# Four graph-attention layers on one core: a bias that rides in with the features, and masks and maxima made for all heads at once

## The chip, the cores and the metric

The kernel runs on one core of a Trainium2 chip. The metric is device time in microseconds of one execution; three timed runs of the kernel before gave 3248.8, 3250.99 and 3244.18 us, median 3248.8. A profile of one execution of the same program shows when each engine was at work: PE (matrix products, with its weight loads PEld), DVE (the vector engine), ACT (pointwise functions), POOL, and SP, whose queue issues nearly all DMAs.

## The reference

128 graphs of 128 nodes with 512 features, and an adjacency matrix for each, pass four graph-attention layers. Each layer normalises and clips its input, and adds its output to it:

```python
h = jnp.maximum(_layernorm(x, axis=-1), 0.0)
x = x + layer(h, adj)
```

All layers score a pair of nodes by a leaky ReLU of the sum of two per-node numbers, mask by the adjacency, take a softmax and sum the nodes' features with it. Layer 1 is two such attentions in a row: the first has 4 heads of 256 features, then a bias and an elu, and the second has one head of 512:

```python
h = jax.nn.elu(gat_layer(x, mask, W1, att_src1, att_dst1, b1, concat=True))
h = gat_layer(h, mask, W2, att_src2, att_dst2, b2, concat=False)
```

Here `gat_layer` returns the attention-weighted sum of `xl = x @ W` plus the bias, and the attention weights of a node sum to 1. Layer 3 has 8 heads of 64 features and a ReLU at the end. All numbers are fp32.

## The kernel before

The 128 graphs are independent, and each is a stream of steps (`graph(b)`, line 1033): layer 0, 1, 2 and 3, then the store. Up to 13 streams are in flight. The program's order is made before the run by the kernel's own planner (`Scheduler`, lines 154 to 312): it holds an estimate of each step's time (`Step.estimate`, line 66), looks for the engine that could start something first, and issues on it the ready step of lowest rank; a rank is the graph's number times the pace plus the step's due time (line 242). A step waits in the planner where its stream needs a buffer that no other has given back (`Take`), where a fork is not over (`Join`), or where a name has not been reached (`Until`). On the chip, each engine then runs its own instructions strictly in that order. A `Group` is a set of instructions of one engine that are issued together.

`setup()` (line 428) loads the weights. Small vectors come by ACT's queue (`few`, line 424), all else by SP's. `fold_w1` (line 516) works out columns of `w1x` that give the scores of layer 1 along with its features; `fold_w2` (line 522) does the same for `w2x` by 16 dot products on DVE, and `fold_w3` for layer 3. `b2` holds layer 1's second bias, spread over all partitions, and is added when the second projection is taken out of PSUM.

Layer 1 (`layer1`, line 797): the clipped input is transposed on PE and copied out by ACT (`ht`). `projected` (line 741) multiplies it by `w1x` in three parts of 344 columns, each of four 128-row chunks; ACT copies each part out of its PSUM bank into `fx` (tile tag `xl`), whose first 8 columns are the scores. When `plus` is given, `projected` has DVE add a row to the part on the way out; before, only the second projection does that, with `b2`. After the softmax, each group of four 128-row pieces of the output (`po`, a PSUM bank) has four matmuls. Then `y` is made from it (lines 852 to 866) in four steps: DVE adds the bias `b1` (one number a partition and piece), which frees the bank; DVE takes the minimum with 0 into a tile `t`; ACT takes the exponential; and DVE takes the maximum of that less 1 and the sum. There are two such groups a graph. `y` is then the left operand of the second projection by `w2x`, in two parts of 257 columns with eight chunks each.

Layer 3 (`layer3`, line 891): a tile `e` of 128 x 1024 holds the scores of 8 heads. For each head one DVE instruction adds the mask and takes the row's maximum into `mx` (lines 928 to 942, two groups of four). POOL and ACT make the softmax's offset from `mx`, and ACT then runs two functions over each head. In the last 5 graphs (`late`) the rows come from PE transposes in PSUM, four heads at a time; in the others by DMA. At the end `t` collects the normalised output.

A matmul of fp32 is two PE instructions with a weight load each. PSUM is 8 banks (`bank`); tile tag `t` has five buffers and is used by layer 0 from its dots to its end, by layer 1 for each group of `y`, by layer 3 at its end, and by `fold_w3`.

Of the kernel before, what the change touches and what calls it, by code (L numbers as in the profile page):

```python
# [9 lines left out]
F32 = mybir.dt.float32  # L10
# [143 lines left out]
class Scheduler:  # L154
# [14 lines left out]
    def give_back(self, *aps):  # L169
        for ap in aps:  # L170
            name = ap.tensor.name
            tag = self.tag_of.pop(name)
            heapq.heappush(self.returned[tag], self.last_use.get(name, 0.0))
# [153 lines left out]
def kernel(  # L327
# [23 lines left out]
    nc = tc.nc  # L351
# [60 lines left out]
    w_src = const.tile([P, D], F32, name="w_src")  # L412
    w_dst = const.tile([P, D], F32, name="w_dst")
    b_l2 = const.tile([P, 1], F32, name="b_l2")
    b1 = const.tile([P, FC], F32, name="b1")
    u1 = const.tile([P, D], F32, name="u1")
    u2 = const.tile([P, D], F32, name="u2")

# [5 lines left out]
    def few(to, values):  # L424
        with nc.allow_non_contiguous_dma(reason="at most 1024 values, once"):
            nc.scalar.dma_start(out=to, in_=values)

    def setup():
        for i, a in enumerate((l0_a1, l0_a2)):
            few(a0[:, :, i], a.rearrange("(c p) o -> p (c o)", p=P))  # L430
        for i, a in enumerate((l1_src1, l1_dst1)):
            few(a1[:, :, i], a.rearrange("h (c p) -> p (h c)", p=P))
        few(b1, l1_b1.rearrange("(c p) -> p c", p=P))

        w0 = []
        for c in range(KC):
            if c % 2 == 0:
                pair = yield tile_of("e3", 3, H3 * P)
                pair = pair.rearrange("p (c f) -> p c f", c=2)
            w0.append(pair[:, c % 2])  # L440
            yield S.dma_start(out=w0[c], in_=l0_w[c * P : (c + 1) * P])
        yield Fork(fold_u(w0))
        yield from load(0)
        for c in range(KC):
            yield S.dma_start(out=w1x[c][:, E1:], in_=l1_w1[c * P : (c + 1) * P])
        yield Fork(fold_w1())
        yield Fork(load_turned(0))
        yield from load(1)
        yield from load(2)
        vecs = []  # L450
        for row in (l1_src2, l1_dst2):
            vecs.append((yield tile_of("x2", 2, E2 + D))[:, :D])
            yield S.dma_start(out=vecs[-1], in_=row[0].partition_broadcast(P))
        for c in range(FC):
            yield S.dma_start(out=w2x[c][:, E2:], in_=l1_w2[c * P : (c + 1) * P])
        yield Fork(fold_w2(vecs), 3)
        yield S.dma_start(out=b2[:, E2:], in_=l1_b2.partition_broadcast(P))
        yield from load(3)
        yield from load(4)
        for t, row in (w_src, l2_src), (w_dst, l2_dst), (b_l2, l2_b), (b_l3[:, 0], l3_batt):  # L460
            yield S.dma_start(out=t, in_=row.partition_broadcast(P))
        yield from load(5)
        for c in range(KC):
            yield S.dma_start(
                out=wpx[c][:, :, E3:],
                in_=l3_wp[c * P : (c + 1) * P].rearrange("p (h k) -> p h k", h=H3),
            )
        wa = yield tile_of("e3", 3, H3 * P)
        wa = wa[:, : H3 * 2 * K3]
        yield S.dma_start(out=wa, in_=l3_watt.rearrange("h k -> (h k)").partition_broadcast(P))  # L470
        yield Fork(fold_w3(wa), 6)
        for b in range(6, min(FLYING + AHEAD, B)):
            yield from load(b)
# [42 lines left out]
    def fold_w1():  # L516
        for w in w1x:
            to = w[:, :E1].rearrange("p (s h) -> p h s", h=H1)
            yield from fold(blocks_of(w[:, E1:]), a1, F1 // P, to)
        sched.reached.add("w1")  # L520

    def fold_w2(vecs):
        for w in w2x:
            for s, vec in enumerate(vecs):
                yield from dot(w[:, E2:], vec, w[:, s : s + 1])
        give_back(*vecs)
        sched.reached.add("w2")

    def fold_w3(wa):
        pairs = wa.rearrange("p (h k) -> p h k", h=H3)  # L530
        for w in wpx:
            for s in range(2):
                prod = yield tile_of("t", 5, D)
                p3 = prod.rearrange("p (h k) -> p h k", h=H3)
                yield V.tensor_tensor(
                    p3, w[:, :, E3:], pairs[:, :, s * K3 : (s + 1) * K3], ALU.mult
                )

                yield V.tensor_reduce(w[:, :, 1 - s], p3, AX.X, ALU.add)
                give_back(prod)  # L540
        give_back(wa)
        sched.reached.add("wp")
# [31 lines left out]
    def blocks_of(t):  # L574

        return [t[:, i : i + P] for i in range(0, t.shape[1], P)]
# [202 lines left out]
    def layer0(xt, mask, late):  # L779
        h = yield from norm_relu(xt)  # L780
        yield Until("u")
        f = yield tile_of("f0", 8, 3)
        yield from dot(h, u1, f[:, 0:1])
        yield from dot(h, u2, f[:, 1:2])
        t = yield tile_of("t", 5, D)
        pa, c, rz = yield from attended(f[:, 0:1], f[:, 1:2], mask, h, late, exact=True)
        give_back(h, f)

        yield A.activation(out=t, in_=pa, func=AF.Exp, scale=rz)
        yield A.activation(out=pa, in_=pa, func=AF.Relu, scale=rz)  # L790
        give_back(c)
        yield V.scalar_tensor_tensor(t, t, 1.0, pa, ALU.min, ALU.add)
        give_back(pa)
        yield V.scalar_tensor_tensor(xt, t, -1.0, xt, ALU.add, ALU.add)
        give_back(t)

    def layer1(xt, mask, late):
# [18 lines left out]
                d = yield from rows_in_dram(fx[:, :Q], H1)  # L816
                yield S.dma_start(out=e.rearrange("p (c f) -> p c f", c=R), in_=d)

        fork = yield from projected(ht, KC, w1x, 3, columns(fx, 3), rows)
        give_back(ht[0])  # L820
        xl = fx[:, E1:]
        yield Join(fork)
# [15 lines left out]
        for g in range(0, FC, 4):  # L838
            po = yield bank()
            yield Group(  # L840
                [
                    T.matmul(
                        po[:, (c - g) * P : (c - g + 1) * P],
                        lhsT=xl[:, c * P : (c + 1) * P],
                        rhs=et[c * P // F1],
                        start=True,
                        stop=True,
                    )
                    for c in range(g, g + 4)
                ]  # L850
            )
            yg = y[:, g : g + 4, :]
            yield V.tensor_tensor(
                yg,
                po.rearrange("p (j q) -> p j q", q=P),
                b1[:, g : g + 4].unsqueeze(2).to_broadcast([P, 4, P]),
                ALU.add,
            )
            give_back(po)

            yg = yg.rearrange("p c q -> p (c q)")
            t = yield tile_of("t", 5, 4 * P)
            yield V.tensor_scalar(t, yg, 0.0, None, ALU.min)
            yield A.activation(out=t, in_=t, func=AF.Exp)
            yield V.scalar_tensor_tensor(yg, t, -1.0, yg, ALU.add, ALU.max)
            give_back(t)
        give_back(fx, et[0])
        yield Until("w2")
        gx = yield tile_of("x2", 2, E2 + D)
# [21 lines left out]
    def layer3(xt, mask, late):  # L891
# [27 lines left out]
            yield S.dma_start(out=e.rearrange("p (c f) -> p c f", c=R), in_=rows)  # L919
        mask3 = mask.rearrange("p (c b) -> p c b", b=Q)  # L920

        for g in range(0, H3, 4):
            part = [heads[:, g + j] for j in range(4)]
            if late:
                pt = yield from spread(f[:, 0, g : g + 4])
                part = pt.rearrange("p (h c b) -> p h c b", h=4, b=Q)
                part = [part[:, j] for j in range(4)]
            yield Group(
                [
                    V.tensor_tensor_reduce(  # L930
                        out=heads[:, g + j],
                        in0=part[j],
                        in1=mask3,
                        scale=1.0,
                        scalar=LOWEST,
                        op0=ALU.add,
                        op1=ALU.max,
                        accum_out=mx[:, g + j : g + j + 1],
                    )
                    for j in range(4)  # L940
                ]
            )
            if late:
                give_back(pt)
        give_back(mask)
        yield G.tensor_tensor(mx, mx, f[:, 1], ALU.add)
        yield A.activation(out=mx, in_=mx, func=AF.Prelu, alpha=SLOPE)
# [10 lines left out]
        else:  # L958
# [5 lines left out]
            )  # L964
            give_back(to)
            et = blocks_of(e)
        t = yield tile_of("t", 5, D)
        for i in range(2):
            pa = yield bank()
            p3 = pa[:, : half * (K3 + 1)].rearrange("p (h k) -> p h k", h=half)  # L970
# [28 lines left out]
    def load(b):  # L999

        xs[b] = xpool.tile([P, D], F32, tag="xt", name="xt")
        yield S.dma_start(out=xs[b], in_=x[b])
        if b % AG == 0:
            adjs[b // AG] = adjp.tile([P, AG, P], I32, tag="at", name="at")
            yield S.dma_start(
                out=adjs[b // AG], in_=adj[b : b + AG].rearrange("g i j -> i g j")
            )
            if b:
                yield Fork(load_turned(b))
        sched.reached.add(("x", b))  # L1010
# [117 lines left out]
```

## Time and profile before

| | |
|---|---|
| timed runs, median (lowest to highest) | 3248.8 us (3244.18 to 3250.99) |
| span of the profiled execution; no other time of it is given | 3245.8 us |
| PE busy | 3191.5 us, 98% |
| DVE busy | 2865.8 us, 88% |
| ACT busy | 2468.6 us, 76% |
| POOL busy | 861.3 us, 27% |
| granted TensorE clock, mean | 0.988 |
| DMA | 462.80 MB, 143 GB/s |

The span runs from the first to the last instruction of the program. Matmuls are pipelined and their ends are modelled, so two that follow each other overlap in the records; the distance of their starts tells what one costs. The same holds for DVE and ACT: an instruction's record overlaps the next one's by some 0.1 us. All the kernel's steps are issued from one line of the planner, 302, so groups of instructions are told apart by the names of the tiles that they write and read, not by the line.

### The profile page before, as it was taken

Reading aid. Unit: us, or ns where it says so; the run is one execution under the profiler, and the core shown is the slowest. Engines: PE = TensorE matmul, PEld = TensorE weight load, DVE = VectorE, ACT = ScalarE, POOL = GpSimd, SP = SyncE. Lnnn points to the kernel's source line nnn. Section 1 sums busy time; section 2 is a strip of 40 time slices with the busy share of each in tenths; the row PEclk is TensorE's granted clock in tenths of the full one; section 3 lists DMA queues with packets and bytes.
Section 4 is the critical chain, followed back from the end, with each engine's and each line's share of the span. In section 5 each row is a group of like instructions: output and inputs, shape, how many; then the busy total and the mean of one; then the engine's idle time right before and its main releaser. Section 6 shows DMA issues by size and latency. Waiting matters only on the chain.

```text
span 3245.8 us, 60294 instructions
## 1 busy us (share of the span) xinstructions
PE 3191.5 (98%) x15362; PEld 2498.0 (77%) x15362; DVE 2865.8 (88%) x11669; ACT 2468.6 (76%) x7221; POOL 861.3 (27%) x2313
## 2 busy tenths in 40 slices
PE   6999999999999999999999999999999999999998
PEld 3777777777777777777777777777777777777786
DVE  5788989999999999989989989989989989989876
ACT  3567777777777777777777778777778777777867
POOL 1122222222222222222222222222222222222222
PEclk6999999999999999999999999999999999999999
DMA  6235565555555555555656555556565555565432
GB/s 172 65 87 141 145 156 146 153 150 149 146 153 151 154 151 147 147 154 151 152 147 153 145 156 152 150 148 154 143 158 152 145 149 154 145 156 149 113 98 69
DMA packets 774259, 462.80 MB, mean 143 GB/s; under 512 B 345496, under 2 KB 706200, under 8 KB 773912
## 3 DMA queue, kind: packets, MB, share of 16 engines
q1 hardware_dynamic: 769736, 458.94, 54.3%
q8 instruction: 123, 2.02, 0.3%
q14 instruction: 224, 1.84, 0.2%
q10 hardware_dynamic: 4176, 0.02, 0.1%
HBM read 300.57 MB, written 158.17 MB: 141 GB/s over the span
## 4 chain that ended last, share of the span: by engine, by line
PE 94%; DVE 2%; DMA 2%; ACT 1%; issue 1%; SPq 0%; POOL 0%; ACTq 0%; DVEq 0%; POOLq 0%
PE bank L302 94%; DVE e L302 1%; ACT e L302 0%; DMA e<-d 0%; SPq L302 0%; DVE t L302 0%; DVE products L302 0%; DVE st L302 0%; DMA xt<-in_x_dram 0%; DVE xt L302 0%; DMA w1x<-in_L_gnn_W_dram 0%; POOL st L302 0%; DVE y L302 0%; ACT h L302 0%; DMA at<-in_adj_dram 0%
## 5 line engine op out<-in xcount | busy, mean ns | idle before, releaser
L302 PE MATMUL bank<-w2x,y 128*128 128x257 f32 x4096 | 968.7, 381 | 0.5 <-DVE y L302 0.5
L302 PE MATMUL bank<-w1x,ht 128*128 128x344 f32 x3072 | 953.4, 454 | 2.6 <-ACT ht L302 2.6
L302 PEld LDWEIGHTS bank<-w2x,y 128*128 128x128 f32 x4096 | 763.4, 190 | 152.8 <-issue 30.7
L302 PEld LDWEIGHTS bank<-w1x,ht 128*128 128x128 f32 x3072 | 571.5, 191 | 260.4 <-issue 13.8
L302 ACT ACTIVATE e<-e,f 128x128 f32<-128x128 f32 x2176 | 707.8, 390 | 5.8 <-POOL st L302 3.0
L302 POOL TENSOR_SCALAR st<-st 128x1 f32<-128x1 f32 x1024 | 312.7, 310 | 1196.3 <-DVE st L302 1019.5
L302 ACT ACTIVATE e<-e,c 128x128 f32<-128x128 f32 x1408 | 534.3, 394 | 113.4 <-DVE c L302 57.5
L302 PE MATMUL bank<-wpx,ht 128*128 128x264 f32 x2048 | 497.1, 386 | 0.3 <-ACT ht L302 0.3
L302 ACT ACTIVATE h<-xt,st 128x512 f32<-128x512 f32 x512 | 411.0, 810 | 77.2 <-POOL st L302 70.5
L302 PEld LDWEIGHTS bank<-wpx,ht 128*128 128x128 f32 x2048 | 387.9, 190 | 98.7 <-issue 23.0
L302 DVE CUSTOM_DVE_ANT_0 e<-e,m 128x128 f32<-128x128 f32 x1496 | 340.5, 285 | 18.1 <-DMA e<-d 17.7
L302 DVE BATCH_NORM_STATS2 st<-xt 128x6 f32<-128x512 f32 x512 | 341.0, 679 | 0.0
L302 POOL TENSOR_TENSOR st<-st,minus_half 128x1 f32<-128x1 f32 x512 | 297.3, 599 | 23.6 <-POOL st L302 0.2
L302 PEld LDWEIGHTS bank<-x,e 128*128 128x128 f32 x1968 | 255.2, 191 | 58.1 <-issue 33.3
L302 PEld LDWEIGHTS bank<-et,xl 128*128 128x128 f32 x2048 | 265.1, 192 | 36.0 <-issue 9.6
L302 PE MATMUL bank<-h,et 128*128 128x512 f32 x512 | 266.6, 604 | 4.2 <-ACT et L302 3.0
L302 PE MATMUL bank<-et,xl 128*128 128x128 f32 x2048 | 269.4, 275 | 0.3 <-DMA et<-exchanged 0.3
L302 ACT COPY xl<-bank 128x344 f32<-128x344 f32 x384 | 167.8, 437 | 116.9 <-PE bank L302 113.8
L302 PE MATMUL bank<-x,e 128*128 128x65 f32 x1968 | 246.4, 268 | 4.9 <-issue 4.9
L302 ACT COPY ht<-bank 128x512 f32<-128x512 f32 x274 | 159.8, 583 | 117.3 <-PE bank L302 116.3
L302 ACT ACTIVATE t<-t 128x512 f32<-128x512 f32 x256 | 160.3, 626 | 96.3 <-DVE t L302 95.4
L302 DVE TENSOR_TENSOR y<-bank,b 128x512 f32<-128x512 f32 x256 | 175.3, 685 | 37.7 <-PE bank L302 37.0
(83 smaller groups left out, 4344.6 us busy)
## 6 DMA issues: line engine op xcount, KB each, us to landing
e<-d SPq DMA_DIRECT2D x123, 512.0 KB
exchanged<-e SPq DMA_DIRECT2D x492, 128.0 KB
et<-exchanged SPq DMA_DIRECT2D x123, 512.0 KB
xt<-in_x_dram SPq DMA_DIRECT2D x128, 256.0 KB
e<-d SPq DMA_DIRECT2D x128, 256.0 KB
out_dram<-xt SPq DMA_DIRECT2D x128, 256.0 KB
exchanged<-e SPq DMA_DIRECT2D x492, 64.0 KB
et<-exchanged SPq DMA_DIRECT2D x123, 256.0 KB
```

Source lines behind the costliest of these rows:

```text
L302: method(*args, **kw)
```

## The change

The bias of layer 1 is added to the features while they are taken out of PSUM, as `b2` is in the second projection; since the attention weights of a node sum to 1, it comes through the weighted sum unchanged. `b1` therefore becomes a row over all partitions, with zeros where the score columns lie. To it 1 is added once, so that the weighted sum is one more than the argument of the elu. From the PSUM bank ACT takes the exponential of the sum less 1, and one DVE instruction takes the larger of the sum and of the exponential capped at 1: this is the elu plus 1. The bank is given back after that instruction. What the 1 adds to the second projection, the column sums of `w2x`, is worked out once on PE by a product with a matrix of ones, and subtracted from `b2`; the name `w2` is reached after that.

In layer 3, one DVE instruction adds the mask to all eight heads (four at a time, from PSUM, in the last 5 graphs), and one reduction then takes all maxima. Tile tag `t` has four buffers in place of five.

```diff
-    b1 = const.tile([P, FC], F32, name="b1")
+    b1 = const.tile([P, E1 + HF], F32, name="b1")
+    nc.gpsimd.memset(b1[:, :E1], 0.0)
+    minus_one = const.tile([P, 1], F32, name="minus_one")
+    nc.gpsimd.memset(minus_one, -1.0)
+    ones = const.tile([P, 1], F32, name="ones")
+    nc.gpsimd.memset(ones, 1.0)
...
-        few(b1, l1_b1.rearrange("(c p) -> p c", p=P))
...
             yield S.dma_start(out=w1x[c][:, E1:], in_=l1_w1[c * P : (c + 1) * P])
+        yield S.dma_start(out=b1[:, E1:], in_=l1_b1.partition_broadcast(P))
         yield Fork(fold_w1())
...
         yield S.dma_start(out=b2[:, E2:], in_=l1_b2.partition_broadcast(P))
+        sched.reached.add("b2")
...
             yield from fold(blocks_of(w[:, E1:]), a1, F1 // P, to)
+        yield V.tensor_scalar(b1[:, E1:], b1[:, E1:], 1.0, None, ALU.add)
         sched.reached.add("w1")
...
         give_back(*vecs)
+        yield Until("b2")
+        for to, *parts in zip(columns(b2, 2), *(columns(w, 2) for w in w2x)):
+            total = yield bank()
+            for g in range(0, FC, 4):
+                yield Group(
+                    [
+                        T.matmul(
+                            total[:, : to.shape[1]],
+                            lhsT=ones.to_broadcast([P, P]),
+                            rhs=parts[c],
+                            start=(c == 0),
+                            stop=(c == FC - 1),
+                        )
+                        for c in range(g, g + 4)
+                    ]
+                )
+            yield V.tensor_tensor(to, to, total[:, : to.shape[1]], ALU.subtract)
+            give_back(total)
         sched.reached.add("w2")
...
-        t = yield tile_of("t", 5, D)
+        t = yield tile_of("t", 4, D)
...
-        fork = yield from projected(ht, KC, w1x, 3, columns(fx, 3), rows)
+        fork = yield from projected(ht, KC, w1x, 3, columns(fx, 3), rows, plus=columns(b1, 3))
...
-            yg = y[:, g : g + 4, :]
-            yield V.tensor_tensor(
-                yg,
-                po.rearrange("p (j q) -> p j q", q=P),
-                b1[:, g : g + 4].unsqueeze(2).to_broadcast([P, 4, P]),
-                ALU.add,
-            )
-            give_back(po)
-
-            yg = yg.rearrange("p c q -> p (c q)")
-            t = yield tile_of("t", 5, 4 * P)
-            yield V.tensor_scalar(t, yg, 0.0, None, ALU.min)
-            yield A.activation(out=t, in_=t, func=AF.Exp)
-            yield V.scalar_tensor_tensor(yg, t, -1.0, yg, ALU.add, ALU.max)
-            give_back(t)
+            t = yield tile_of("t", 4, 4 * P)
+            yield A.activation(out=t, in_=po, func=AF.Exp, bias=minus_one)
+            yg = y[:, g : g + 4, :].rearrange("p c q -> p (c q)")
+            yield V.scalar_tensor_tensor(yg, t, 1.0, po, ALU.min, ALU.max)
+            give_back(po, t)
...
-        for g in range(0, H3, 4):
-            part = [heads[:, g + j] for j in range(4)]
+        for g in range(0, H3, 4 if late else H3):
+            n = 4 if late else H3
+            own = part = heads[:, g : g + n].rearrange("p h c b -> p c h b")
             if late:
                 pt = yield from spread(f[:, 0, g : g + 4])
-                part = pt.rearrange("p (h c b) -> p h c b", h=4, b=Q)
-                part = [part[:, j] for j in range(4)]
-            yield Group(
-                [
-                    V.tensor_tensor_reduce(
-                        out=heads[:, g + j],
-                        in0=part[j],
-                        in1=mask3,
-                        scale=1.0,
-                        scalar=LOWEST,
-                        op0=ALU.add,
-                        op1=ALU.max,
-                        accum_out=mx[:, g + j : g + j + 1],
-                    )
-                    for j in range(4)
-                ]
-            )
+                part = pt.rearrange("p (h c b) -> p c h b", h=4, b=Q)
+            wide = mask3.unsqueeze(2).to_broadcast([P, R, n, Q])
+            yield V.tensor_tensor(own, part, wide, ALU.add)
             if late:
                 give_back(pt)
+        yield V.tensor_reduce(mx, heads, AX.XY, ALU.max)
         give_back(mask)
```

More of the change, by code (lines that the diff above doesn't have):

```diff
@@ L532, in fold_w3 @@
             for s in range(2):
-                prod = yield tile_of("t", 5, D)
+                prod = yield tile_of("t", 4, D)
                 p3 = prod.rearrange("p (h k) -> p h k", h=H3)
@@ L966, in layer3 @@
             et = blocks_of(e)
-        t = yield tile_of("t", 5, D)
+        t = yield tile_of("t", 4, D)
         for i in range(2):
```

## The prediction

> **What bounds the kernel now.** I read the page's busy table and slices first, to see whether one engine is full all the way, then busy time by stretch, then who PE waits for, then the costliest groups, and last the timeline where PE is not full.
>
> ```profile
> span 3245.8 us, 60294 instructions
> PE 3191.5 (98%) x15362; PEld 2498.0 (77%) x15362; DVE 2865.8 (88%) x11669; ACT 2468.6 (76%) x7221; POOL 861.3 (27%) x2313
> PE   6999999999999999999999999999999999999998
> PEclk6999999999999999999999999999999999999999
> PE 94%; DVE 2%; DMA 2%; ACT 1%; issue 1%; SPq 0%; POOL 0%; ACTq 0%; DVEq 0%; POOLq 0%
> ```
>
> PE is at nine tenths or more in every slice but the first and the last, and the chain that ended last is 94% PE. Busy PE alone proves little, so the starts have to be looked at: between 310 and 3180 us matmuls of one kind start at a fixed distance (217 ns for 257 columns, 289 ns for 344), and the sum of such distances over all matmuls is 3177 us. The other 69 us of the span are at its two ends. The stretches show it (columns: length, then busy time and instructions of each engine, clock, DMA share, GB/s):
>
> ```profile
> 0.00:43.00 43.00, 34.76 (x121) 24.65 (x121) 16.53 (x58) 13.41 (x27) 4.01 (x18) 0.70 1.02 304
> 43.00:76.00 33.00, 10.84 (x22) 4.47 (x22) 28.25 (x86) 10.40 (x22) 7.51 (x20) 0.50 0.17 27
> 76.00:106.00 30.00, 26.68 (x90) 16.98 (x90) 18.38 (x59) 18.00 (x54) 4.53 (x13) 0.90 0.20 50
> 106.00:310.00 204.00, 199.83 (x934) 154.60 (x932) 168.90 (x665) 137.10 (x404) 49.73 (x120) 1.00 0.38 99
> 310.00:3180.00 2870.00, 2867.78 (x13903) 2255.55 (x13904) 2596.19 (x10633) 2242.30 (x6569) 782.46 (x2102) 1.00 0.57 148
> 3180.00:3246.00 66.00, 51.57 (x298) 41.70 (x297) 37.55 (x172) 47.36 (x147) 13.02 (x40) 0.92 0.16 57
> ```
>
> In 2870 us PE is idle 2.2 us; DVE, third column of the five, is idle 274 us and ACT 628 us. Only the first 106 us and the last 66 us leave PE anything to wait for. From 43 to 76 us PE has 10.8 us of work, at half clock, and DVE 28.3 of 33. So the question of this change is whether PE gets more work, whether the start or the end grows, and whether DVE still feeds PE in the middle.
>
> **The change part by part.** Its own units are these rows of the groups:
>
> ```profile
> L302 PE MATMUL bank<-w2x,y 128*128 128x257 f32 x4096 | 968.7, 381 | 0.5 <-DVE y L302 0.5
> L302 DVE SCALAR_TENSOR_TENSOR y<-t,y 128x512 f32<-128x512 f32 x256 | 176.0, 688 | 9.8 <-ACT t L302 6.0
> L302 DVE TENSOR_TENSOR y<-bank,b 128x512 f32<-128x512 f32 x256 | 175.3, 685 | 37.7 <-PE bank L302 37.0
> L302 ACT COPY xl<-bank 128x344 f32<-128x344 f32 x384 | 167.8, 437 | 116.9 <-PE bank L302 113.8
> L302 DVE TENSOR_SCALAR t<-y 128x512 f32<-128x512 f32 x256 | 107.8, 421 | 3.9
> L302 DVE TENSOR_TENSOR x<-bank,b 128x257 f32<-128x257 f32 x256 | 105.0, 410 | 19.6 <-PE bank L302 16.4
> ```
>
> Records of one engine overlap, so I price by the median distance of starts where instructions follow without a gap: bias add on y 0.603 us, minimum 0.338, closing instruction 0.602 (0.658 for the same kind with a PSUM operand, row xt<-bank,c,xt), 257-wide add from PSUM 0.323, ACT copy of 344 0.342, Exp of 512 0.536 from SBUF and 0.586 from PSUM with a column operand. The masks of layer 3 are told by the timeline:
>
> ```profile
> 3229.75 0.29 DVE L302 CUSTOM_DVE_ANT_0 e<-bank,m 128x128 f32<-128x128 f32 x1 [1.89 <-PE bank L302]
> 3229.97 0.08 DVE L302 DVE_READ_ACCUMULATOR2_ANT f<- 128x1 f32 x1
> 3229.97 0.28 DVE L302 CUSTOM_DVE_ANT_0 e<-bank,m 128x128 f32<-128x128 f32 x1
> ```
>
> One starts 0.21 us after the other, accumulator read included.
>
> *Layer 1, per graph.* Removed from DVE: 2 x (0.603 + 0.338 + 0.602) = 3.09 us. Added: 2 x 0.658 = 1.32, and three 344-wide adds from PSUM, between 0.323 at 257 and 0.603 at 512, on the line 0.42 each, 1.26. ACT loses 3 x 0.342 and gains 2 x 0.05: 0.93 less.
>
> *Layer 3, per graph.* Removed: 8 x 0.212 = 1.70 us. Added: one add over 1024 and one reduction over 1024. At 512 both kinds take 0.60 (t<-wpx,e and its reduction wpx<-t); the 1024-wide transpose takes 1.16. Two of these are 2.33 us, so layer 3 gets 0.63 us dearer: eight instructions that added and took the maximum in one pass become two passes.
>
> The Trainium skill, "VectorE: DVE Perf Modes", under "Rules for kernel authors", says to cut the number of DVE instructions, which would make eight into two a gain; the same table says to expect a reduction at its slowest rate and to restructure. The rows decide for the second: by the first rule alone this part would save something of the 1.70 us, by the rows it costs 0.63.
>
> *DVE together:* 3.09 + 1.70 out, 1.32 + 1.26 + 2.33 in: +0.12 us per graph, 15 us over 128. It is spread over 2870 us in which DVE idles 274. I cost it at zero in the middle; the cover is PE's queue of other graphs' work, and without it 15 us would show. The new adds wait for PE at the head of DVE's queue, as x<-bank,b does now (16.4 us for 256); behind them are other graphs' masks and norms. In exchange the wait on y (37.0) moves to ACT, and the wait of r on ACT's xl (46.6) becomes DVE's own order.
>
> *Buffers.* A bank of the 8 is held from its first matmul to its last reader; for the y groups that is 2.8 us on average, and becomes about 4.5 (matmuls 1.0, wait 1.05, Exp 0.68, wait 1.03, closing 0.73). All groups together hold about two banks at a time now; this adds 0.13. Tile t goes from five buffers to four: counted along the timeline never more than four are in use, and four for 3.6% of the time. Both zero.
>
> *Two sums of w2x's rows on PE, once.* 2 halves x 8 chunks x 2 passes = 32 matmuls of 257 columns. At full clock 16 take 3.47 us (118.96 to 122.43 in the timeline), so 6.9 us; at half clock, which 43 to 76 us has, 13.8. They can start when the last dot of w2x is done at 51.7 us, and their result is wanted by the first w2x matmul at 112.3. PE idles 22 us between 43 and 76, so I take zero, and keep 0 and 13.8 as ends.
>
> The Trainium skill, "TensorE: Matmul & The Clock Gate", Part 1, puts the return to full clock at about 3.4 us of sustained work; the trace has 2.9 us from 75.8 and 3.8 us from 95.3. By the page's figure the sums would take about 8.6 us, an estimate.
>
> *Start, DMAs and DVE.* b1 becomes a 512 KB broadcast on SP's queue behind w1x, ahead of at_t, x(1), x(2) and w2x; the small transfer on ACT's queue goes (1.85 us of issue, nobody waits). Up to 43 us the DMA engines are full at 304 GB/s: 1.7 us for everything behind, and the chain runs through DMAs until 46 us, so I take 1.7 (ends 0 and 1.7). DVE gets one pass over b1's 1024 (0.338 at 512, so about 0.7) and two subtractions (0.323 each) in or ahead of a stretch where it is 86% busy: 1.35 (ends 0 and 1.35). Each subtraction waits for its sum at the head of DVE's queue, with layer 0 and at_t's transposes behind it. Between 0 and twice 3.5 us (the half clock's surplus on 16 matmuls) I take 1.0, near the low end, since DVE has 5 us idle there anyway; this wait is the same cost as the 13.8 seen from DVE, not a further end.
>
> *End.* In the last graph the masks of layer 3 run 3229.75 to 3231.5, 1.75 us; two adds of 0.6 and the reduction of 1.15 make 2.35: +0.6 (ends 0 and 1.5, were two graphs' delays to add up). Layer 1 is over by 3176 us, so its shorter chain is worth nothing here.
>
> *Sum:* 1.7 + 1.35 + 1.0 + 0.6 = 4.65 us on a span of 3245.8, 3250.5. The page gives no other time of that execution; the three timed runs have median 3248.8, 3.0 above the span. On that footing I predict 3253.5, 0.14% more. About 0.2%, 6.5 us, is what can be told from no change.
>
> **The rivals.**
> *The sums are not hidden* (slower). The groups of eight matmuls stand in front of the short transposes and products of layer 0 in PE's in-order queue, and DVE stalls behind its subtractions, so that layer 1 starts later than 75.8 us. For it: PE's queue is fixed before the run, and the clock is at half there. Against: 22 us idle. Price 6.9 to 13.8 in place of my 1.0: 3259.4 to 3266.3. It decides as soon as 2.9 us of them show.
> *DVE no longer feeds PE* (slower). 90.5% busy between 310 and 3180 becomes 91%, with 384 evacuations from PSUM more. If a tenth of ACT's 113.8 us of waits for them came through to PE, 11.4 us: 3264.9. Against: PE's waits there are 3.1 us in all with 274 us of DVE idle.
> *The start gets shorter* (faster). at_t's transposes come at 69.2 us though its transfers were issued by 50; another order of DVE's queue could have layer 1 begin up to some 10 us earlier, and the shorter chain of y could take the 4.2 us that PE idles from 106 to 310. All of it would give 3239.3, half 3246.4. Against: nothing in the change touches those steps' own needs.
>
> **How the numbers follow.** Forecast 0.48, sums shown 0.34, DVE 0.06, shorter start 0.12. Slower by over 0.2%: most of the second, the third, a little of the first, 0.38; faster: most of the last, 0.10; within: 0.52. The low end is the 4.2 us gained and nothing lost, 3244.6; the high end all upper bounds, 1.7 + 1.35 + 13.8 + 1.5 = 18.35, 3267. The forecast's own range is 3249 to 3257.
>
> **What the changed profile would show.** Right: 32 more matmuls with w2x as the moving operand, between 52 and 76 us; PE in the middle stretch as full as now; DVE busy 2880 us, ACT 2350; the first stretch of full PE beginning some 4 us later; the reduction at about 1.2 us. Wrong: PE idle in slices 4 to 39, by DVE xl or ACT t; the w1x matmuls starting later than 82 us; an order that brings layer 1 before 70 us; 1024-wide instructions at more than 1.3 us.

## The result, and the profile after

The changed kernel takes 3333.3 us (median of 4 runs, 3324.8 to 3335.9) where the kernel before takes 3248.0 (4 runs, 3244.2 to 3251.0): 1.0256 times as long, 95% interval 1.0239 to 1.0272. The prediction was 3253.5 with a range to 3267.0. It was wrong by about 80 us, and outside its range.

The page of the changed kernel answers the first fence of the prediction:

```profile
span 3333.4 us, 58253 instructions
PE 3231.8 (97%) x15394; PEld 2506.3 (75%) x15394; DVE 2866.1 (86%) x9757; ACT 2304.5 (69%) x6837; POOL 832.5 (25%) x2316
PE   7999999999999999999999999999999999999998
PEclk7999999999999999999999999999999999999999
PE 29%; DVE 29%; DMA 29%; SPq 5%; ACT 3%; issue 3%; POOL 2%; DVEq 0%; ACTq 0%; POOLq 0%
```

Two lines look nearly unchanged, and one has turned over. PE is still at "nine tenths or more" in the same slices, and DVE's busy time is 2866.1 us where it was 2865.8. But the chain that ended last was 94% PE and is now 29% PE, 29% DVE and 29% DMA. A slice of 83 us prints a 9 when PE loses 2 us of it; losses of that size, in most slices, are the result. Busy time by stretch shows where (columns: length, then busy time and instructions of PE, PEld, DVE, ACT and POOL, clock, DMA share, GB/s):

```profile
0.00:43.00 43.00, 32.85 (x121) 22.84 (x122) 15.69 (x56) 12.48 (x28) 4.10 (x21) 0.74 1.01 305
43.00:76.00 33.00, 18.34 (x50) 9.52 (x49) 29.03 (x89) 10.67 (x21) 6.81 (x19) 0.71 0.26 41
106.00:310.00 204.00, 200.33 (x920) 155.20 (x919) 159.56 (x565) 126.08 (x372) 48.50 (x118) 0.98 0.40 96
310.00:3180.00 2870.00, 2813.87 (x13468) 2186.70 (x13467) 2531.64 (x8678) 2036.17 (x6057) 733.54 (x2048) 1.00 0.56 145
3180.00:3333.00 153.00, 139.09 (x735) 113.58 (x734) 103.83 (x289) 101.48 (x311) 33.64 (x96) 0.93 0.24 76
```

From 310 to 3180 us PE did 13468 matmuls where it did 13903, and was idle 56 us where it was idle 2. To see the loss without the overlap of records I took the distance from each matmul's start to the next, less the median distance of its kind in the whole kernel. Summed by stretch, this excess went from 44.5 to 36.2 us up to 106 us, stayed at 7 from there to 310, went from -9 to 77 in the middle and from 17 to 20 at the end. The start and the end, on which the prediction spent its sum, are not where the time went. The middle is, at a granted clock of 1.00. (The last stretch is 153 us long here and 66 before, since the changed kernel ends later.)

What DVE waits for in that stretch has changed kind. Waits of DVE from 310 to 3180 us (total us, times, longest), the kernel before:

```profile
DVE c L302 <- ACT e L302: 72.6, 129, 1.2
DVE e L302 <- DMA row<-d: 29.9, 38, 2.2
DVE e L302 <- DMA e<-d: 11.6, 17, 1.6
```

and the changed kernel, the two that lead its list:

```profile
DVE e L302 <- DMA e<-d: 114.6, 73, 3.6
DVE e L302 <- DMA row<-d: 92.5, 84, 3.0
```

These are score rows that come back from DRAM spread over the partitions: `e<-d` where a layer has several heads, `row<-d` where it has one. 41.5 us of such waits became 207.1. An instruction that waits at the head of DVE's queue holds up everything behind it. ACT feels it: its idle time ahead of the functions that it runs over score tiles (the third number behind the bar), ended mostly by DVE, nearly trebled, before and changed:

```profile
L302 ACT ACTIVATE e<-e,c 128x128 f32<-128x128 f32 x1408 | 534.3, 394 | 113.4 <-DVE c L302 57.5
L302 ACT ACTIVATE e<-e,c 128x128 f32<-128x128 f32 x1408 | 538.2, 395 | 318.8 <-DVE c L302 181.6
```

And PE's largest wait of the whole span is for a copy-out of ACT that came late:

```profile
PE bank L302 <- ACT ht L302: 44.0, 50, 2.1
```

The chain that ended last shows one such loop, in order of time (start, length, what). Pieces under 0.1 us are left out, and at the dots more issues of SP's queue:

```profile
1023.10 0.44 DVE xl L302
1023.56 0.21 DVE r L302
1023.83 0.57 DVE y L302
1024.40 0.13 DVE r L302
1024.55 0.50 SPq L302
...
1027.76 5.70 DMA row<-d
1033.48 0.39 DVE e L302
1033.88 0.60 DVE y L302
1034.52 3.01 DMA d<-r
1037.55 6.00 DMA e<-d
1043.58 1.23 DVE e L302
```

Read it downwards: DVE makes a row of scores (`r`), SP's queue issues, the row lands 5.7 us later, DVE uses it, two more transfers take 9 us, and DVE's wide add of layer 3's masks (`e`, 1.23) is what comes last. No piece of these 20 us of the chain is PE's. Several graphs are tied into one chain because DVE takes their steps in one fixed order.

The instructions themselves cost what was predicted:

```profile
L302 DVE TENSOR_TENSOR xl<-bank,b 128x344 f32<-128x344 f32 x384 | 192.4, 501 | 23.3 <-PE bank L302 22.0
L302 DVE SCALAR_TENSOR_TENSOR y<-t,bank 128x512 f32<-128x512 f32 x256 | 172.5, 674 | 7.5 <-ACT t L302 7.0
L302 DVE TENSOR_REDUCE f<-e 128x8 f32<-128x1024 f32 x128 | 154.4, 1206 | 0.3
L302 DVE TENSOR_TENSOR e<-e,m 128x1024 f32<-128x1024 f32 x123 | 150.2, 1221 | 121.8 <-DMA e<-d 121.4
```

By distance of starts: 0.423 us for the add on 344 columns (predicted 0.42), 0.594 for the closing instruction (0.658), 1.142 and 1.129 for the wide add and the reduction (2.33 for both). The 121.8 us of idle time ahead of the 123 wide adds is new: ahead of the old mask instructions on `e`, layer 1's among them, it was 18.1.

### The profile page after: what moved, and what is told of

The parts are those of the page before. It is cut to its first block, busy times and chain, and to the rows that moved or that the text cites. A ratio compares the mean times of both kernels' runs of the same rounds, so it can differ in the third digit from the quotient of the medians.

```text
span 3333.4 us, 58253 instructions
## 1 busy us (share of the span) xinstructions
PE 3231.8 (97%) x15394; PEld 2506.3 (75%) x15394; DVE 2866.1 (86%) x9757; ACT 2304.5 (69%) x6837; POOL 832.5 (25%) x2316
## 4 chain that ended last, share of the span: by engine, by line
PE 29%; DVE 29%; DMA 29%; SPq 5%; ACT 3%; issue 3%; POOL 2%; DVEq 0%; ACTq 0%; POOLq 0%
PE bank L302 29%; DMA e<-d 10%; DMA row<-d 8%; DVE e L302 7%; DMA d<-r 6%; SPq L302 5%; DVE products L302 3%; DVE xt L302 3%; DVE f L302 3%; DVE st L302 3%; DMA dealt<-e 2%; DVE y L302 2%; DVE t L302 2%; DVE xl L302 2%; POOL st L302 1%
## 5 line engine op out<-in xcount | busy, mean ns | idle before, releaser
L302 ACT ACTIVATE e<-e,f 128x128 f32<-128x128 f32 x2176 | 724.0, 392 | 10.7 <-DVE c L302 10.1
L302 POOL TENSOR_SCALAR st<-st 128x1 f32<-128x1 f32 x1024 | 296.0, 294 | 1355.5 <-DVE st L302 1077.8
L302 DVE TENSOR_TENSOR e<-e,m 128x1024 f32<-128x1024 f32 x123 | 150.2, 1221 | 121.8 <-DMA e<-d 121.4
L302 DVE CUSTOM_DVE_ANT_1 e<-row,m 128x128 f32<-128x128 f32 x361 | 138.0, 382 | 122.3 <-DMA row<-d 101.8
L302 ACT ACTIVATE t<-bank,minus_one 128x512 f32<-128x512 f32 x256 | 173.4, 678 | 56.7 <-PE bank L302 56.1
L302 DVE TENSOR_TENSOR xl<-bank,b 128x344 f32<-128x344 f32 x384 | 192.4, 501 | 23.3 <-PE bank L302 22.0
```

The lines of the kernel that those rows point to most:

```text
L302: method(*args, **kw)
```

## Experiments

Three theories stood at the outset. **A**: layer 1's new structure costs the time (bank held longer, four buffers for `t`, DVE waiting for PE's projection). **B**: layer 3's two wide instructions cost it (more DVE time, maxima later). **C**: the planner, given other steps, draws another order of all instructions, and that order is worse; the new instructions matter little by themselves. Under C two forms were told apart later: **C1**, the order is bad because the planner believes that transfers land too early; **C2**, an order is a draw, and the one before was a good one. Ratios are to the kernel before, run on the same chip beside it, with 95% intervals; times in us of different groups of runs can differ by 0.3% for that reason. None of these kernels leaves out or changes any part of the computation.

**The two parts alone.** The first run has the diff without layer 3's masks and maxima, the second only these.

> Layer 1's part alone, with its wide b1, the sums of w2x's rows and four t buffers; layer 3 keeps its eight instructions that add and take the maximum in one pass. The whole change costs about 85 us, with DVE's busy time unchanged at 2866 us; PE, full in the middle before, waits some 2 us in each slice there. Theory A, structure of layer 1 (the first projection is now taken out by DVE and the y bank is held through the exponential): this kernel carries most of the 85 us, 3310 to 3335. Theory B, structure of layer 3 (an instruction over all eight heads waits for the whole transfer and is followed by a reduction before anything else can go on): about before, 3245 to 3258. Theory C, the order (no instruction is to blame; the planner laid DVE's readers of a transfer right at the time at which it believes that to land, and DVE waits for the real landing): any time from 3245 to 3335, and the wait of DVE on e<-d and row<-d goes with it, under 80 us in all where the time is near before and over 150 where it is near the changed kernel.

> Layer 3's part alone; layer 1, b1 and t as before. Theory A: about before, 3245 to 3258. Theory B: most of the 85 us, 3310 to 3335. Theory C: any time between, with DVE's waits on e<-d and row<-d going with it; the planner has the same believed end for it as for before.

Measured: layer 1 alone 3316.1 us, 1.0190 (1.0166 to 1.0213); layer 3 alone 3368.7, 1.0356 (1.0330 to 1.0382). Layer 3 alone is dearer than the whole change, and the parts do not add up: 1.9% and 3.6% against 2.6% together. Neither A nor B can give that by itself, since each would leave its cost in the sum. C had a miss too: it allowed at most 3335 us, and waits for score rows of over 150 us in such slow runs, where they were 122.5 and 131.6 us. In the first run DVE has 50 us less work than before (2815.0 us) and ACT 158 less, and PE still loses 37 us in the middle.

**Instruction and order apart.** Here the planner is told the old prices, buffers read and written, of the steps that are put in, so that it draws the order of before; then the reverse.

```diff
+def priced_as(step, other):
+    step.busy, step.delay = other.busy, other.delay
+    step.reads, step.writes = other.reads, other.writes
+    return step
...
-            yield Group(
+            four = Group(
...
+            elif g == 0:
+                own = heads.rearrange("p h c b -> p c h b")
+                made = [V.tensor_tensor(own, own, wide.to_broadcast([P, R, H3, Q]), ALU.add)]
+            else:
+                made = [V.tensor_reduce(mx, heads, AX.XY, ALU.max)]
+            yield priced_as(Group(made), four)
```

> Layer 3's new instructions in the order of before, exactly: the one add over eight heads stands where the first four of the old instructions stood, the reduction where the second four stood, and the planner is told the old cost, reads and writes. DVE gets 0.57 us more to do in each graph, 73 us in all, and idles 380. Theory B (the instructions themselves cost): as slow as layer 3 alone, up to 3335. Theory C: within 15 us of before, PE's waits in the middle still under 10 us.

> The reverse: the old eight instructions in the order that the planner makes for layer 3's new ones, four where the add stands and four where the reduction stands, but for the last graphs. Theory B: as before, 3245 to 3255. Theory C: as layer 3 alone, within 10 us of it, whatever that is, and with its waits of DVE on e<-d.

Measured: the new instructions in the old order 3283.4 us, 1.0091 (1.0073 to 1.0109); the old eight instructions in the order drawn for the new ones 3346.0, 1.0280 (1.0258 to 1.0301). In the traces of the first run and of before every engine runs the same instructions in the same sequence, but for the masks and maxima; the second shares its order with layer 3 alone except in the last graphs. So 2.8% of layer 3's 3.6% come with no new instruction at all, and 0.9% come with no new order. C's "within 15 us of before" was missed by the first, and its "within 10 us" of layer 3 alone by the second (22.7 us below); B is further off in both. The middle stretch of the latter run, same columns as above, in which the order is all that differs from before:

```profile
310.00:3180.00 2870.00, 2801.05 (x13383) 2182.30 (x13382) 2516.41 (x10326) 2154.47 (x6356) 763.38 (x2037) 0.99 0.56 144
```

PE is idle 69 us there, more than in the changed kernel, with before's own instructions.

**The kernel before, redrawn.** One constant of the planner was moved in the kernel before, `PATIENCE`: on DVE and ACT the planner takes the step of lowest rank among those that could start up to so many us after the soonest. The instructions stay the same. The first run has .2, the second .4.

```diff
-PATIENCE = .3
+PATIENCE = .2
```

> The kernel before with one number of its planner changed: PATIENCE 0.2 in place of 0.3, so that DVE and ACT are laid out by a slightly different rule. No instruction is added, dropped or changed. The last runs left the order as the cause of most of the time; two theories of it remain. C1, the order of the changed kernel is bad in a nameable way: the planner believes that transfers land sooner than they do, and leaves DVE's readers no margin; then this order, whose margins in the plan are those of before (0.5 us on layer 3's scores on average, 1.1 on row), runs as before, 3245 to 3262. C2, the order of before is one lucky draw among many: its constants suit exactly its instructions, and any other order, also of the same instructions, lands somewhere between 3260 and 3370.

> The same with PATIENCE 0.4; the plan's mean margin on layer 3's scores is 0.13 us here, against 0.58 before. C1: slower than the kernel with 0.2, by tens of us, with DVE's wait on e<-d over 50 us. C2: anywhere from 3260 to 3370, and not ordered by that margin.

Measured: with .2 3276.8 us, 1.0069 (1.0054 to 1.0084); with .4 3443.7, 1.0582 (1.0566 to 1.0598). An untouched set of instructions loses up to 190 us by its order, more than C2's range allowed. That .4 is the slower of the two is what C1 said; that .2 is slower than before is not. Two waits of the second one in the middle stretch, one of DVE and one of PE:

```profile
DVE e L302 <- DMA row<-d: 136.7, 53, 6.1
PE bank L302 <- DMA et<-exchanged: 85.1, 29, 4.5
```

**The changed kernel, redrawn.** Told that a transfer of SP's queue lands 0.5 us later than the planner's figure; with PATIENCE 0; with PATIENCE .2.

```diff
-            return busy, (2.2 if moved > 16384 else 1.3)
+            return busy, (2.2 if moved > 16384 else 1.3) + 0.5
```

> The changed kernel with the planner told that every transfer lands 0.5 us later; its believed end grows by 16 us. C1: DVE's waits on e<-d and row<-d, 223 us in the changed kernel, halve or better, and the time comes down to 3255 to 3285. C2: another draw, 3260 to 3370, with no reason to be nearer to before.

> The changed kernel with PATIENCE 0; the plan's margin on layer 3's scores is 0.05 us, as little as in the changed kernel. C1: within 25 us of the changed kernel. C2: another draw, 3260 to 3370.

> The changed kernel, same instructions, PATIENCE .2 in place of .3: another order. If the order of before is one lucky draw and any other scatters (C2), 3260 to 3400 us, not tied to 3333. If the changed instructions have a floor of their own (A or B), nothing below 3316 us, since no order so far of either part alone or both was below that except the one planned for the old instructions.

Measured: 3317.0 us, 1.0189 (1.0171 to 1.0207); 3403.4, 1.0449 (1.0428 to 1.0471); 3282.9, 1.0107 (1.0084 to 1.0131). The later landing did what C1 says to the waits, 207.1 us of score rows became 57.2, and yet only 0.7%, some 22 us, came back; other waits had taken their place, `c` on ACT's `e` (59.1 us) and `xl` on PE (55.6). That speaks against C1 as the whole story, and so does PATIENCE 0, which C1 put within 25 us of the changed kernel and which lies above the range of C2 as well. PATIENCE .2 brought back 1.5%, some 48 us, with 141.2 us of waits for score rows left.

**The layer-1 part, redrawn.**

> The layer-1 part alone (old masks and maxima in layer 3), with the planner told that a transfer lands 0.5 us later. DVE has about 50 us and ACT about 160 us less work than before. By A (layer 1's longer bank hold, fewer buffers and the wait of DVE for PE cost time in any order) it stays at 3305 to 3330 us. By C2 it is a new draw, anywhere in 3245 to 3400. At 3250 or below the layer-1 part would be as good as before or better in some order, and A would be out.

> The layer-1 part alone with PATIENCE .2 in place of .3. By A 3305 to 3330 us again; by C2 a new draw, 3245 to 3400 us, and unlike the run with the later landing.

> The layer-1 part alone, landings told 0.75 us later in place of 0.5 (which took 3254.7). By C1 about the same, 3245 to 3260 us; by C2 another draw, 3260 to 3400.

Measured: told 0.5 us later 3254.7 us, 1.0018 (1.0008 to 1.0027); PATIENCE .2 3360.8, 1.0350 (1.0309 to 1.0391); told 0.75 us later 3281.0, 1.0070 (1.0055 to 1.0085), where C1 expected 3260 at most. The first settles A: with its 384 new adds, four buffers, longer bank hold and the sums at the start, layer 1's part can run with PE full. Its middle stretch, and then its largest waits of DVE there:

```profile
310.00:3180.00 2870.00, 2865.01 (x13865) 2249.90 (x13864) 2541.46 (x10482) 2124.42 (x6216) 801.70 (x2096) 1.00 0.58 147
```

```profile
DVE f L302 <- PE bank L302: 52.9, 115, 1.1
DVE xl L302 <- PE bank L302: 51.7, 115, 2.3
DVE y L302 <- ACT t L302: 47.7, 63, 1.9
DVE c L302 <- ACT e L302: 38.9, 92, 1.4
DVE e L302 <- DMA row<-d: 14.9, 23, 1.9
```

DVE idles even longer than in the kernel before, 329 us against 274, but two of its three longest waits are for PE. While PE is full, waiting for it costs nothing; an engine that waits for a transfer may be what empties PE.

**Both parts, in the orders of the layer-1 runs.** Layer 3's new instructions were put into two of those orders, in the way of the second experiment: that of layer 1 alone (3316.1 us without them) and that with landings told 0.5 us later (3254.7).

> Both parts of the change, nothing left out of the computation, in the order that the planner drew for the layer-1 part alone (it is told the old prices of layer 3's masks and maxima, as in the run with layer 3 in the order of before). The layer-1 part alone in this order took 3316 us. If an order costs what it costs and layer 3's new instructions add their own delay on top (theory C), the 0.9% of that earlier run should come again: 3338 to 3352 us. If the delay of layer 3's maxima is hidden once PE already has gaps, it stays at 3310 to 3325. Below 3300 would speak for the two parts helping each other, above 3370 for B: layer 3's instructions being dear by themselves.

> The whole change, in the order planned for the layer-1 part alone with landings 0.5 us later (3254.7 us without layer 3's part); the planner is told the old prices of layer 3's masks and maxima. If the new instructions delay each graph's maxima and the order has no slack for it, as in the run of layer 3 in the order of before (+27 us), 3275 to 3290 us. If that order hides them, 3252 to 3262 us: then the change as a whole costs next to nothing and all 85 us are the order's. Above 3310 us would make them dearer than any run here shows.

Measured: 3337.9 us, 1.0278 (1.0263 to 1.0293); and 3272.8, 1.0047 (1.0030 to 1.0064). Every engine's sequence is the same in the trace as in the run that lent it, but for the masks and maxima. The first adds 0.9% again, as C had it; the second lies between the two ranges that were given for it, near the upper. The second kernel has the instructions of the changed kernel, engine by engine (the totals in the span lines differ by the waits on semaphores, which follow the order), and so its page, laid beside that of the changed kernel, shows what an order is worth:

```profile
span 3270.7 us, 57972 instructions
PE 3211.0 (98%) x15394; PEld 2511.4 (77%) x15394; DVE 2870.8 (88%) x9757; ACT 2329.6 (71%) x6837; POOL 895.6 (27%) x2316
PE 72%; DVE 13%; DMA 7%; ACT 4%; issue 2%; SPq 2%; POOL 1%; ACTq 0%; DVEq 0%; POOLq 0%
```

15394 matmuls, 9757 on DVE, 6837 on ACT, 2316 on POOL, as in the changed kernel, and the times stand as 1.0256 to 1.0047: 2.1%, some 68 us. The middle stretch, and then DVE's waits for score rows in it:

```profile
310.00:3180.00 2870.00, 2857.93 (x13811) 2244.26 (x13810) 2582.45 (x8825) 2106.31 (x6196) 812.43 (x2089) 1.00 0.58 147
```

```profile
DVE e L309 <- DMA row<-d: 24.9, 31, 2.0
DVE e L309 <- DMA e<-d: 14.3, 15, 2.1
```

**The control.** The kernel before with landings told 0.5 us later.

> The kernel before, told that transfers land 0.5 us later. If the later landing makes orders better in general (C1), 3240 to 3255 us and hardly any wait of DVE for score rows. If an order is a draw (C2), 3260 to 3400 us, as with the other two changes of a constant in this kernel.

Measured: 3295.9 us, 1.0120 (1.0102 to 1.0138), and 83.7 us of waits for score rows where the order of before has 41.5. The constant that gave the layer-1 part its good order made this kernel's order worse. C1 falls as a rule. C2 stands, with a wider scatter than it foretold; it says that the order decides, not why.

**All runs together.** Price of layer 3's two instructions, in four orders, each the ratio of two kernels that share it, in the second row but for the last graphs (intervals added in quadrature, the last three from two ratios):

| order drawn for | old eight | new two | difference |
|---|---|---|---|
| the kernel before | 1 | 1.0091 | +0.9% (0.7 to 1.1) |
| layer 3 alone | 1.0280 | 1.0356 | +0.7% (0.4 to 1.1) |
| layer 1 alone | 1.0190 | 1.0278 | +0.9% (0.6 to 1.1) |
| layer 1, landings +0.5 us | 1.0018 | 1.0047 | +0.3% (0.1 to 0.5) |

Price of the order, for one set of instructions each (us):

| instructions | orders |
|---|---|
| before | 3248, 3277, 3296, 3444 |
| layer 1 alone | 3255, 3281, 3316, 3361 |
| the whole change | 3273, 3283, 3317, 3333, 3338, 3403 |

The three ranges overlap. The order of before is the best of its four, so the 2.6% of the result compare a good order with a middling one. Over draws these runs can't tell the change from before; only the held orders price a part of it.

Over the profiles of all 17 kernels PE's busy time in the middle stretch falls as DVE's waits for score rows rise, with a correlation of -0.81. It is a symptom that goes with the loss, not a measure of it: against before, the run with 57.2 us of such waits lost 38 us of PE, and one with 99.4 (the kernel before with PATIENCE .2) lost 15.

## Why the prediction was wrong

**The step that failed** is the one that costed DVE at zero in the middle: "the cover is PE's queue of other graphs' work, and without it 15 us would show". It took the 274 us in which DVE idled for slack, and PE's 98% for a property of the kernel. Both were properties of one order. The change alters steps of every graph, so the planner drew the order of all instructions anew, and the new order makes DVE wait for transfers 207 us instead of 41.5. For this the sum had no term. With the instructions held and the order changed, the difference is 68 us, four fifths of the 83 (2.56%) by which the kernel became slower. Layer 1's part, in the best of its four orders, costs 0.18%.

**A second term was mis-sized.** Layer 3's two passes were priced right, 2.27 us measured against 2.33, in place of 1.70, so 73 us more DVE work over 128 graphs. But the prediction netted it against layer 1's 3.09 - 2.58 us and hid the rest. In four orders this part costs 0.3 to 0.9%, 9 to 30 us, by itself. A likely reason, argued from the chain and not tried, is that the maxima come 0.57 us later in a loop with transfers in it, and that layer 1's saving lies at another place. The conflict of rules in the Trainium skill, "VectorE: DVE Perf Modes", "Rules for kernel authors", comes out as the rows said: two instructions took 2.27 us where eight took 1.70, because the reduction was a pass of its own.

**The start** was costed at 1.7 + 1.35 + 1.0 = 4.05 us. The first `w1x` matmul began at 76.8 us where it began at 75.8, and PE had made up for it by 106 us: its excess is 8.3 us less, of which the added matmuls, 6.7 us at full clock, are the larger part. The three terms were too high by 3 to 6 us, in a start that was redrawn too. The rival of sums that are not hidden is refuted by that: they ran from 46.9 to 58.5 us, and the run of 3254.7 us has them too. The rival of a shorter start did not come either: layer 1 began 1.0 us later, not earlier. One reading was off, though no term hung on it: the 2.9 us before the full clock were counted from 75.8 us, but PE had been at its transposes since 73.7, so that row has 4.9 us.

**The end** was costed at 0.6; PE's excess after 3180 us rose by 3.6, in an end that another order had arranged.

**DVE's and ACT's totals.** 2880 and 2350 us were predicted for DVE and ACT, 2866.1 and 2304.5 measured. Why they fell short was not looked into. The totals say little about a change of this kind: the two kernels on either side of the 68 us have DVE at 2866 and 2871.

**The rivals.** "DVE no longer feeds PE" had a chance of 0.06 and a price of 11.4 us. It was the nearest in kind, and wrong in its cause and size: not ACT's former 113.8 us of waits for PE coming through with the new adds (`xl` waited 7.6 us in the middle), but DVE waiting for transfers. The prediction's own sign for it, "PE idle in slices 4 to 39", came true as to the idling, not as to `xl` or `t`, and could hardly be seen in a row of nines; the chain (94% PE to 29%) told it at once. The rival that was missing is "the order is drawn anew, and PE starves a little everywhere".

**What was right**: the price of each new instruction to within 0.07 us, the harmlessness of four buffers, bank hold and sums (they are all in the run of 3254.7 us). The forecast of +4.65 us also lies near the 0.18%, 5.9 us (2.6 to 8.8), of layer 1's part in its best order, but that is luck: it is one draw of four, and the start, which made up most of the 4.65, did not cost it. For the whole change in its best order it is 15 us (10 to 21).

**What stays open.** Why one order starves PE and another doesn't was not reduced to a number that could be read before the run. The chain and the waits show the loop of DVE, SP's queue and transfers, but taking its waits away in one run (207.1 to 57.2 us) brought back some 22 us only. Nor was any order found in which the change beats the kernel before: in the six tried it costs 0.5 to 4.5% of the best order of before.

## What to carry to other kernels

When a static order is planned from estimates, a change of one step redraws everything, and the scatter between orders of the same instructions (here 3248 to 3444 us) can be many times the effect of the change; price the redraw as a term of its own, with the bound that redraws of the old kernel give, and compare changes over several draws or in a held order. A busy share of 98% and an engine's idle time are not reserves: look at what that engine waits for. While PE was full, DVE's waits for it were harmless; waits for transfers grew in most of the slow orders here, though not in every one (57.2 us in the run of 3317.0 us). Two instructions in place of eight are no gain where the eight did both jobs in one pass.

## What the runs showed of the hardware that was not expected

The 32 matmuls of the sums were feared at half clock, since PE had 0.50 from 43 to 76 us. In the changed kernel all but the first few ran at the full one. Busy time from 47 to 59 us, columns as in the stretches above, first of the changed kernel and then of the kernel before, shows that the granted clock was 0.95 and 0.50, and the sums' records have a median of 380 ns; the same kind of matmul for the second projection has a mean of 382 over the whole kernel.

```profile
47.00:59.00 12.00, 8.89 (x34) 6.07 (x32) 11.59 (x34) 2.05 (x3) 1.19 (x4) 0.95 0.39 62
```

```profile
47.00:59.00 12.00, 0.71 (x2) 0.36 (x2) 10.89 (x36) 2.48 (x6) 2.36 (x6) 0.50 0.28 45
```

PE's busy time from 43 to 76 us rose by 7.5 us there, not by 13.8. In the next 17 us, with PE busy 6.75 us in single pieces, the clock was 0.58.

This can't be counted on. In the run of layer 1 alone the same 32 matmuls took from 47.4 to 60.6 us at a granted clock of 0.73 (47 to 61 us), their records have a median of 534 ns, and PE's busy time from 43 to 76 us rose by 9.3 us. Pauses of PE do not tell the two runs apart by their length: both have pauses of up to 0.77 us between the groups. In the changed kernel the clock held through them; in the other run it rose at 51.3 us and was back at 0.50 from 54.7 to 58.1. Why was not tried.
